# Gates, means and rates land on 64 partitions, and ScalarE copies them to the other 64

## The chip, the cores and the metric

The kernel runs on one core of one Trainium2 chip. Five engines work side by side, each with its own queue of instructions, which it takes strictly in order: TensorE (PE, with its weight loads as PEld), VectorE (DVE), ScalarE (ACT), GpSimd (POOL) and SyncE (SP), which here issues the DMAs. They wait for one another by semaphores. The metric is the device time of one execution in microseconds (us); the time of a kernel is the median of its runs. Profiles come from one profiled execution.

## What is computed

One layer on an image batch x of shape (2, 128, 256, 256), float32: a windowed attention (8x8 windows, keys from 12x12 windows, relative positions, a fixed mask that leaves every second row and column), then a mixture of eight experts for each pixel, of which the two likeliest count.

```
x = x + attention(layernorm over channels(x), W_qkv, W_out, rel_height, rel_width)
t = pixels of x as tokens of 128 channels
n = layernorm(t)
p = softmax(n @ router_w + router_b)                # 8 experts
top_p, top_i = top 2 of p, divided by their sum
t = t + sum over the two of top_p * (n @ expert_w[top_i] + expert_b[top_i])
```

The mask makes the four pixel parities of an image independent, so the attention runs on four "planes" of each strip.

## The kernel before

The image is cut into strips of 8 rows, 64 strips in all. A strip is worked on in four planes, one for each parity of row and column, so the main loop runs over 256 planes, `n`. In each plane it computes the attention of one plane, projects the next one, and does the expert layer for one chunk of 512 pixels (two image rows, "row" in the code) of the strip before. The order of the instructions on all engines is written out by hand in this loop: what stands first in the program stands first in its engine's queue.

**The expert layer of a chunk takes three planes.** In plane n, `norms` squares the chunk (ScalarE, L537), sums it by matmuls (L543), turns the sums (VectorE, L552) and computes the rates (L192 to L199 with two small ScalarE steps, L196 and L197). `route` then finds the two experts and their shares, the gates; its softmax exponential is on ScalarE (L581), and VectorE's next step, L590, needs it. Gates, the means and the rates of the next layer norm have one number for each pixel, but every channel, so every partition, needs them. `spread` writes them to a small DRAM tile `gd` (L622), and DMAs read them back to all 128 partitions by broadcast: `fetch_rstd` (tile `rb`, L628), `fetch_means` (tile `sb`, L657) and `Experts.fetch` (tiles `gb`, L652), each 128 partitions x 512 numbers, 256 KB. In the plane after that, `means` makes xs = x + means (L662), `times` multiplies xs by each gate (L668; experts 5 and 7 on GpSimd, the others on VectorE), and `product` multiplies by the expert's weights on TensorE (L677), all eight summed in one accumulator. `end` adds the accumulator to x (L683).

**The order around the copies.** A gate's buffer comes free when its last reader is done. `fetch` marks that by writing one column of it, on ScalarE or VectorE (L649, L651), and the DMA waits for that mark. In the order of the loop, ScalarE has: the exponential of the scores L462, the values L318, the mark of gate 7, the keys L394 and L404, the queries L410, the two squares L537, the mark for loading x (L116), L196 and L197, the mark of gate 4, L581, the mark of gate 5. SP has, in each plane: gate 7, `gd`, the value rows (L329), `rb`, `sb`, the value windows `vwin` (L341, two DMAs to 60 partitions each, one in each half of the partitions), gates 0, 1, 2, x, gate 3, the finished chunk to DRAM (L715), gates 4, 6, 5. GpSimd has: a copy of one column that makes it wait for gate 6's multiply (`behind`, L672), the multiply of gate 5, the layer norm of a row (`ln1`, L236), sometimes a copy of a halo row (L210), the multiply of gate 7. TensorE has, from the score matmuls (L437, L454) on: the projections of the next plane (L310, L369, L383, L408), products 4, 6, 7, 5 of the chunk before, the attention (L475, L485), the sums L543, products 0, 1, 2, the output projection L513, product 3.

**The start.** For the first six planes (`FILL`) there are no or few expert chunks, and the order is a little different.

**The finish.** `finish_last` does the last four chunks together, on a shorter path: one route for all four (L798 to L849), gates fetched to 128 partitions into buffers of x that are free, multiplies on VectorE, two of eight on GpSimd (L760), products into four parts of one PSUM tile `accs` (L767), adds (L878, L882) and stores.

**Alignment.** `nc.tensor.addr_align` puts idle instructions in TensorE's stream, so that the borders of its instruction blocks (256 instructions) fall at chosen places of the loop.

Of the kernel before, what the change touches and what calls it, by code (L numbers as in the profile page):

```python
# [52 lines left out]
def kernel(  # L53
# [571 lines left out]
    def fetch_rstd(gd, nm):  # L625

        rb = gates.tile([P, NT * P], F32, tag="rb", name=f"rb{nm}", bufs=2)
        nc.sync.dma_start(rb, to_all(gd, E + 1))  # L628
        return rb

    def to_all(gd, j):

        return gd[j * NT : (j + 1) * NT].rearrange("r k -> (r k)").partition_broadcast(P)

    class Experts:
# [7 lines left out]
        def fetch(self, e, eng):  # L643
# [6 lines left out]
            else:  # L650
                eng.memset(self.gb[e][:, 0:1], 0.0)  # L651
            nc.sync.dma_start(self.gb[e], to_all(self.gd, e))  # L652

        def fetch_means(self):

            self.sb = gates.tile([P, NT * P], F32, tag="sb", name="sb%d_%d" % self.at, bufs=1)
            nc.sync.dma_start(self.sb, to_all(self.gd, E))  # L657

# [27 lines left out]
    class NoExperts:  # L686
        def fetch(self, e, eng):
            pass

# [32 lines left out]
    def finish_last(ex, nxt, gated):  # L722
# [27 lines left out]
        def multiply(at, row):  # L750
# [6 lines left out]
            for e in range(E):  # L757
                xe = work.tile([P, CH], F32, tag="xe", name=f"xel{row}_{e}", bufs=8)
                eng = nc.gpsimd if e in (2, 5) and row < 4 else nc.vector
                eng.tensor_tensor(xe, xs, gb[e], ALU.mult)  # L760
                out.append(xe)
            return out

        def products(acc, xes):
            order = (0, 1, 3, 2, 4, 6, 5, 7)
            for j, e in enumerate(order):
                nc.tensor.matmul(  # L767
                    acc, lhsT=ew[:, e, :], rhs=xes[e], start=(j == 0), stop=(j == E - 1)
                )
# [22 lines left out]
        for e in (0, 1, 2, 3, 4, 6, 5, 7):  # L792
            nxt.times(e, nc.gpsimd)
        for e in (0, 1, 2, 3, 4, 6, 5, 7):
# [70 lines left out]

        accs = ps_att.tile([P, 4, CH], F32, tag="att", name="accs")
        todo = [f] + rows
        before = nxt
        for row, at in enumerate(todo):
# [3 lines left out]
            if row == 0:  # L873
                before.end()
                store(*to_store.pop())
            else:
                src = rows_of(*todo[row - 1])
                nc.vector.tensor_add(src, accs[:, (row - 1) % 4], src)  # L878
                store(*todo[row - 1])
            products(accs[:, row % 4], xes)  # L880
        src = rows_of(*todo[-1])
        nc.vector.tensor_add(src, accs[:, (len(todo) - 1) % 4], src)  # L882
        store(*todo[-1])
# [95 lines left out]
    with tc.manual_schedule(engines={ET.PE, ET.DVE, ET.Activation, ET.Pool, ET.SP}):  # L979
        for n in range(n_planes):  # L980
# [11 lines left out]

            usual = n > 6 and row_at(n - 1) is not None
            if usual:
                nc.tensor.addr_align(BLOCK, offset=BLOCK - FIRST_LIMIT)
# [11 lines left out]
            next(ahead, None)  # L1007
            nxt.fetch(7, nc.scalar)
            if gated:
                f, c, made = gated  # L1010
                gd = spread(f, c, made[0], f"_{n}")
                new = Experts(*f, gd) if f else new
# [11 lines left out]
            for e in (4, 6, 7, 5):  # L1024
                ex.product(e)
            if n >= 6 and not usual:
                nc.tensor.addr_align(BLOCK, offset=SUMS_AT)


            f = (i - 1, pl) if 0 < i <= len(strips) else None  # L1030
            c = row_at(n)
            if f or c:
                room = None
# [26 lines left out]
            load_x((n + 9) // 4, (n + 9) % 4, paced=True)  # L1060
            new.fetch(3, dve)
            while to_store:
                store(*to_store.pop())
# [3 lines left out]
            ex.product(1)  # L1067
            ex.product(2)
            new.fetch(4, nc.scalar)
            nxt.behind(6)  # L1070
            nxt.times(5, pool)
# [74 lines left out]
```

## Time and profile before

| what | value |
|---|---|
| median of three runs | 4292.7 us |
| lowest and highest | 4290.45, 4301.58 us |
| the profiled execution | 4302.19 us |
| its span, first to last instruction | 4300.4 us |
| mean granted TensorE clock | 0.994 |
| DMA share of the middle slices | 0.78 to 0.79 |
| data moved by DMA | 1022 MB, mean 238 GB/s |
| DMAs of gates, means, rates | 2008, 251, 249, 256 KB each |
| median from issue to landing | 5.7, 4.3, 3.5 us |
| mean of one multiply of a gate, VectorE, GpSimd | 685, 1272 ns |

Times in the profile are microseconds unless marked ns. A line of the timeline has: start, duration, engine, line of the kernel, operation, output and inputs, partitions x elements, and how many instructions are merged (x8); a bracket at the end gives the idle time of the engine just before and what ended it ("issue": nothing that the profile shows). A DMA line gives the tile, the queue (SPq), how many, the size and the median time from issue to landing. Matmuls of float32 are shown as two instructions each, and matmuls overlap, so a busy TensorE is not TensorE at its peak. Busy shares are averages over the whole span.

### The profile page before, as it was taken

To read this page: it belongs to the slowest core of one execution; us is meant where nothing else is said; L and a number is where in the kernel's file an instruction comes from. 1 tells how busy PE (TensorE), PEld (TensorE's weight loads), DVE (VectorE), ACT (ScalarE), POOL (GpSimd) and SP (SyncE) were. 2 spreads that over 40 slices of the span, in tenths; PEclk is the share of its full clock that TensorE was granted. 3 is DMA by queue.
4 is the path that set the end of the run, shared out by engine and by line. 5 is a ranking of instruction groups with operands and counts; after the bars stand their busy time and mean duration, and the time that the engine had idled before them with its cause. 6 is when DMAs were issued, how large, how long until landed. Compare 5 with 4: busy or idle time off the path is not lost.

```text
span 4300.4 us, 224047 instructions
## 1 busy us (share of the span) xinstructions
PE 4214.7 (98%) x94273; PEld 2457.6 (57%) x94273; DVE 3786.3 (88%) x11752; ACT 1315.5 (31%) x3750; POOL 1093.2 (25%) x1125
## 2 busy tenths in 40 slices
PE   7999999999999999999999999999999999999997
PEld 5555555555555555555555555555555555555553
DVE  5888898998988888998898888989898888888887
ACT  3333333332323232333333333323233333333320
POOL 1222222222222222222222222222222222222222
PEclk9999999999999999999999999999999999999999
DMA  4777777877787877887778787787778787777776
GB/s 141 228 248 238 245 242 244 244 245 243 240 248 233 251 235 234 247 244 242 247 239 249 237 249 239 246 245 244 238 243 249 234 249 238 243 234 247 232 217 198
DMA packets 824576, 1022.15 MB, mean 238 GB/s; under 512 B 137634, under 2 KB 409634, under 8 KB 823594
## 3 DMA queue, kind: packets, MB, share of 16 engines
q1 hardware_dynamic: 822864, 1007.52, 75.7%
q8 instruction: 769, 12.60, 1.3%
q14 instruction: 213, 1.74, 0.1%
q10 hardware_dynamic: 730, 0.29, 0.0%
HBM read 863.78 MB, written 143.75 MB: 234 GB/s over the span
## 4 chain that ended last, share of the span: by engine, by line
PE 97%; issue 1%; DVE 1%; DMA 1%; SPq 0%; ACT 0%; POOL 0%; POOLq 0%; DVEq 0%
PE acc L677 41%; PE att L454 8%; PE att L485 7%; PE pv L310 7%; PE plt L543 6%; PE pu L369 5%; PE po L513 5%; PE pk L383 5%; PE pq L408 5%; PE att L437 4%; PE att L475 3%; DMA gl<-gd_l 1%; PE accs L767 0%; PE pltn L253 0%; DMA xt<-in_x_dram 0%
## 5 line engine op out<-in xcount | busy, mean ns | idle before, releaser
L677 PE MATMUL acc<-xe,ew 128*128 128x512 f32 x4016 | 1880.8, 599 | 10.2 <-issue 8.9
L677 PEld LDWEIGHTS acc<-xe,ew 128*128 128x128 f32 x4016 | 740.9, 190 | 913.0 <-issue 856.3
L668 DVE TENSOR_TENSOR xe<-xs,gb 128x512 f32<-128x512 f32 x1500 | 927.6, 685 | 8.6
L672 POOL COPY last<-xe 128x1 f32<-128x1 f32 x250 | 45.9, 184 | 3042.7 <-DVE gb L651 3042.7
L668 POOL TENSOR_TENSOR xe<-xs,gb 128x512 f32<-128x512 f32 x508 | 645.4, 1272 | 12.2 <-DMA gb<-gd 10.7
L454 PE MATMUL att<-qs,kcol 32*60 32x32 f32 x32768 | 393.9, 222 | 25.2 <-issue 24.7
L454 PEld LDWEIGHTS att<-qs,kcol 32*60 32x60 f32 x32768 | 388.1, 126 | 29.7 <-issue 29.0
L236 POOL TENSOR_TENSOR xn<-xt,rb 128x512 f32<-128x512 f32 x249 | 374.4, 1504 | 87.5 <-DMA rb<-gd 74.2
L485 PEld LDWEIGHTS att<-pT,vwin 64*32 64x32 f32 x32768 | 350.8, 105 | 48.6 <-issue 11.1
L485 PE MATMUL att<-pT,vwin 64*32 64x32 f32 x32768 | 348.7, 201 | 9.1 <-issue 8.4
L462 ACT ACTIVATE pT<-att 128x1024 f32<-128x1024 f32 x256 | 262.0, 1023 | 269.4 <-PE att L454 269.3
L310 PE MATMUL pv<-wt,xn 128*128 128x128 f32 x2048 | 300.3, 290 | 0.0
L537 ACT ACTIVATE sq<-xt 128x512 f32<-128x512 f32 x501 | 290.2, 630 | 0.0
L357 DVE STREAM_TRANSPOSE au<-auT 128x512 f32<-128x512 f32 x256 | 269.5, 1053 | 8.8
L373 DVE STREAM_TRANSPOSE uT<-pu 128x512 f32<-128x512 f32 x256 | 183.2, 716 | 105.2 <-PE pu L369 102.1
L394 ACT COPY kcol<-pk 128x560 f32<-128x560 f32 (+2 forms) x344 | 183.0, 532 | 290.5 <-PE pk L383 287.7
L513 PE MATMUL po<-o,wt 128*128 128x512 f32 x512 | 262.1, 593 | 4.5 <-ACT kcol L404 2.1
L369 PE MATMUL pu<-xn,wrel 128*128 128x512 f32 x512 | 266.0, 601 | 0.0
L408 PE MATMUL pq<-xn,wt 128*128 128x512 f32 x512 | 261.8, 592 | 1.6 <-issue 1.6
L383 PE MATMUL pk<-xn,wt 128*128 128x512 f32 (+2 forms) x528 | 262.4, 580 | 0.0
L310 PEld LDWEIGHTS pv<-wt,xn 128*128 128x128 f32 x2048 | 251.0, 193 | 10.6 <-DVE xn L236 0.2
L437 PEld LDWEIGHTS att<-au,keys 32*64 32x64 f32 x8192 | 116.0, 131 | 195.5 <-PE po L513 189.2
(2445 smaller groups left out, 4935.1 us busy)
## 6 DMA issues: line engine op xcount, KB each, us to landing
gb<-gd SPq DMA_DIRECT2D x2008, 256.0 KB, 5.7
vwin<-vrows SPq DMA_DIRECT2D x512, 240.0 KB, 4.8
xt<-in_x_dram SPq DMA_DIRECT2D x256, 256.0 KB, 6.6
out_dram<-xt SPq DMA_DIRECT2D x256, 256.0 KB, 6.0
sb<-gd SPq DMA_DIRECT2D x251, 256.0 KB, 4.3
rb<-gd SPq DMA_DIRECT2D x249, 256.0 KB, 3.5
vrows<-vr SPq DMA_DIRECT2D x168, 256.0 KB, 3.9
vrows<-vr SPq DMA_DIRECT2D x160, 128.0 KB, 3.4
```

The lines of the kernel that those rows point to most:

```text
L236: eng.tensor_tensor(xn[i % 2][:, :, :, k, 1 : PC + 1], ln1_src(i, k).rearrange("p (y j x) -> p y x j", y=2, x=2), rb.rearrange("p (y j x) ...
L310: nc.tensor.matmul(pv[:, j * P : (j + 1) * P], lhsT=xp[:, k, 1 : PC + 1], rhs=wv, start=True, stop=True,)
L369: nc.tensor.matmul(pu, lhsT=wrel, rhs=inner, start=True, stop=True)
L383: nc.tensor.matmul(pk[:, : m * PC], lhsT=wk, rhs=xp[:, part[0] : part[0] + m, 1 : PC + 1], start=True, stop=True,)
L408: nc.tensor.matmul(pq, lhsT=wq, rhs=inner, start=True, stop=True)
L437: nc.tensor.matmul(sc[rows, h].rearrange("p (t w z) -> p t w z", w=2, z=16)[:, :, w], lhsT=keys[hp, turn, w], rhs=au[hp, half * NP + w : ( ...
L454: nc.tensor.matmul(sc[rows, h, 32 * t : 32 * t + 32], lhsT=kk[hp, half * HP + t, 0:NK], rhs=qs[hp, m0 : m0 + 2].rearrange("p m a s -> p (m ...
L485: nc.tensor.matmul(av[hp, half, 32 * t : 32 * t + 32], lhsT=vv[rows, t, hp], rhs=pT[rows, h, 32 * t : 32 * t + 32], start=True, stop=True,)
L513: nc.tensor.matmul(po, lhsT=wo, rhs=state["o"].rearrange("p f z -> p (f z)"), start=True, stop=True)
L537: nc.scalar.activation(sq, src, AF.Square)
L668: eng.tensor_tensor(self.xe[e], self.xs, self.gb.pop(e), ALU.mult)
L677: nc.tensor.matmul(self.acc, lhsT=ew[:, e, :], rhs=self.xe.pop(e), start=(e == 0), stop=not self.xe)
```

## The change

- `to_all` gets a count, and two helpers are new: `fetch_half` reads to partitions 0 to 63 alone (128 KB), and `other_half` copies those 64 partitions to the other 64 on ScalarE. Rates, means and gates of the main loop go this way. The finish still fetches its gates to 128 partitions.
- The copies are put into ScalarE's order by hand: gate 3 behind the mark of gate 7; gates 4, 6, 5 behind the queries, ahead of the squares; means, rates and gate 7 behind the mark for loading x; gate 0 behind L197, then the mark of gate 4, gates 1 and 2, ahead of L581.
- In the finish, all multiplies are on VectorE, both those of the last regular chunk (before: all eight on GpSimd) and those of the last rows (before: two of eight on GpSimd); the products are in the order of the experts; and each row's products have a PSUM tile of their own in place of a part of `accs`.
- The alignment at a plane's start is kept in one more plane (250).

```diff
@@ -625,12 +625,20 @@
     def fetch_rstd(gd, nm):
 
         rb = gates.tile([P, NT * P], F32, tag="rb", name=f"rb{nm}", bufs=2)
-        nc.sync.dma_start(rb, to_all(gd, E + 1))
+        fetch_half(rb, gd, E + 1)
         return rb
 
-    def to_all(gd, j):
-
-        return gd[j * NT : (j + 1) * NT].rearrange("r k -> (r k)").partition_broadcast(P)
+    def to_all(gd, j, count=P):
+
+        return gd[j * NT : (j + 1) * NT].rearrange("r k -> (r k)").partition_broadcast(count)
+
+    def fetch_half(tile_, gd, j):
+
+        nc.sync.dma_start(tile_[0:SLOT], to_all(gd, j, SLOT))
+
+    def other_half(tile_):
+
+        nc.scalar.copy(tile_[SLOT:], tile_[0:SLOT])
 
     class Experts:
 
@@ -649,12 +657,20 @@
                 eng.copy(self.gb[e][:, 0:1], onesm[:, 0:1])
             else:
                 eng.memset(self.gb[e][:, 0:1], 0.0)
-            nc.sync.dma_start(self.gb[e], to_all(self.gd, e))
+            fetch_half(self.gb[e], self.gd, e)
+
+        def double(self, e):
+
+            other_half(self.gb[e])
 
         def fetch_means(self):
 
             self.sb = gates.tile([P, NT * P], F32, tag="sb", name="sb%d_%d" % self.at, bufs=1)
-            nc.sync.dma_start(self.sb, to_all(self.gd, E))
+            fetch_half(self.sb, self.gd, E)
+
+        def double_means(self):
+
+            other_half(self.sb)
 
         def means(self):
 
@@ -685,6 +701,12 @@
 
     class NoExperts:
         def fetch(self, e, eng):
+            pass
+
+        def double(self, e):
+            pass
+
+        def double_means(self):
             pass
 
         def fetch_means(self):
@@ -756,16 +778,14 @@
             out = []
             for e in range(E):
                 xe = work.tile([P, CH], F32, tag="xe", name=f"xel{row}_{e}", bufs=8)
-                eng = nc.gpsimd if e in (2, 5) and row < 4 else nc.vector
-                eng.tensor_tensor(xe, xs, gb[e], ALU.mult)
+                nc.vector.tensor_tensor(xe, xs, gb[e], ALU.mult)
                 out.append(xe)
             return out
 
         def products(acc, xes):
-            order = (0, 1, 3, 2, 4, 6, 5, 7)
-            for j, e in enumerate(order):
+            for e in range(E):
                 nc.tensor.matmul(
-                    acc, lhsT=ew[:, e, :], rhs=xes[e], start=(j == 0), stop=(j == E - 1)
+                    acc, lhsT=ew[:, e, :], rhs=xes[e], start=(e == 0), stop=(e == E - 1)
                 )
 
         gd = spread(f, None, made[0], "_c")
@@ -790,7 +810,9 @@
         nxt.means()
         ex.end()
         for e in (0, 1, 2, 3, 4, 6, 5, 7):
-            nxt.times(e, nc.gpsimd)
+            if e > 2:
+                nxt.double(e)
+            nxt.times(e, nc.vector)
         for e in (0, 1, 2, 3, 4, 6, 5, 7):
             nxt.product(e)
 
@@ -863,7 +885,7 @@
             2, gds[1], [gates.tile([P, CH], F32, tag="gb", name=f"gl2_{e}", bufs=8) for e in range(E)]
         )
 
-        accs = ps_att.tile([P, 4, CH], F32, tag="att", name="accs")
+        accs = []
         todo = [f] + rows
         before = nxt
         for row, at in enumerate(todo):
@@ -875,11 +897,12 @@
                 store(*to_store.pop())
             else:
                 src = rows_of(*todo[row - 1])
-                nc.vector.tensor_add(src, accs[:, (row - 1) % 4], src)
+                nc.vector.tensor_add(src, accs[row - 1], src)
                 store(*todo[row - 1])
-            products(accs[:, row % 4], xes)
+            accs.append(mm_tile(f"accl{row}"))
+            products(accs[row], xes)
         src = rows_of(*todo[-1])
-        nc.vector.tensor_add(src, accs[:, (len(todo) - 1) % 4], src)
+        nc.vector.tensor_add(src, accs[-1], src)
         store(*todo[-1])
 
     n_planes = 4 * len(strips)
@@ -990,8 +1013,8 @@
 
 
 
-            usual = n > 6 and row_at(n - 1) is not None
-            if usual:
+            late = n == 6 or n > 6 and row_at(n - 1) is None
+            if n > 6 and (not late or row_at(n - 2) is not None):
                 nc.tensor.addr_align(BLOCK, offset=BLOCK - FIRST_LIMIT)
 
 
@@ -1006,6 +1029,7 @@
             next(score, None)
             next(ahead, None)
             nxt.fetch(7, nc.scalar)
+            nxt.double(3)
             if gated:
                 f, c, made = gated
                 gd = spread(f, c, made[0], f"_{n}")
@@ -1023,12 +1047,14 @@
                 next(ahead, None)
             for e in (4, 6, 7, 5):
                 ex.product(e)
-            if n >= 6 and not usual:
+            if late:
                 nc.tensor.addr_align(BLOCK, offset=SUMS_AT)
 
 
             f = (i - 1, pl) if 0 < i <= len(strips) else None
             c = row_at(n)
+            for e in (4, 6, 5):
+                nxt.double(e)
             if f or c:
                 room = None
                 if filling:
@@ -1059,6 +1085,10 @@
                 next(ahead, None)
             load_x((n + 9) // 4, (n + 9) % 4, paced=True)
             new.fetch(3, dve)
+            new.double_means()
+            if row:
+                other_half(row[2])
+            nxt.double(7)
             while to_store:
                 store(*to_store.pop())
             next(ahead, None)
@@ -1066,7 +1096,10 @@
             made = next(norm, None)
             ex.product(1)
             ex.product(2)
+            new.double(0)
             new.fetch(4, nc.scalar)
+            new.double(1)
+            new.double(2)
             nxt.behind(6)
             nxt.times(5, pool)
             if row:
```

## The prediction

> **What bounds the kernel now.** I read the chain of waits first, then the waits, one regular plane on each engine, and the DMA table.
>
> ```profile
> span 4300.4 us, 224047 instructions
> PE 4214.7 (98%) x94273; PEld 2457.6 (57%) x94273; DVE 3786.3 (88%) x11752; ACT 1315.5 (31%) x3750; POOL 1093.2 (25%) x1125
> ...
> PE 97%; issue 1%; DVE 1%; DMA 1%; SPq 0%; ACT 0%; POOL 0%; POOLq 0%; DVEq 0%
> ...
> gb<-gd SPq DMA_DIRECT2D x2008, 256.0 KB, 5.7
> vwin<-vrows SPq DMA_DIRECT2D x512, 240.0 KB, 4.8
> ```
>
> TensorE is the bound, so no removed DMA shortens the path directly. The starts of L437 lie 16.245 us apart in an undisturbed plane. Over the 241 planes between 130 and 4100 us the excess over 16.245 sums to 54 us, with 96 planes over by more than 0.05. Three planes, each with a granted clock of 0.5 for 3.4 us, make 9.5 us of it. Much of the rest is idle time that always falls at the same matmul, ended by "issue":
>
> ```profile
> 2031.23 0.36 PE L454 MATMUL att<-qs,kcol 32*60 32x32 f32 x17
> 2031.78 1.31 PE L454 MATMUL att<-qs,kcol 32*60 32x32 f32 x111 [0.18 <-issue]
> ```
>
> Always with 111 left in L454, 21 in L485 or 5 in L677: edges of instruction blocks (the instruction queue moved 769 packets of 16 KB), whose fetch shares the DMA engines with the gates. So 54 us is the most that steady planes could give back. The question is what the new ScalarE work costs. Here is its row of one plane, without what lies between:
>
> ```profile
> 2000.28 1.02 ACT L462 ACTIVATE pT<-att 128x1024 f32<-128x1024 f32 x1 [0.84 <-PE att L454]
> ...
> 2005.48 0.18 ACT L116 COPY xt<-onesm 128x1 f32<-128x1 f32 x1
> 2012.78 0.18 ACT L196 ACTIVATE r__121_38773<-plg 128x8 f32<-128x8 f32 x1 [7.12 <-DVE plg L195]
> 2012.99 0.21 ACT L197 ACTIVATE r__121_38773<-r__121_38773 128x8 f32<-128x8 f32 x1
> 2013.10 0.17 ACT L649 COPY gb<-onesm 128x1 f32<-128x1 f32 x1
> 2015.29 0.23 ACT L581 ACTIVATE lg<-lg 128x32 f32<-128x32 f32 x1 [2.01 <-DVE lg L580]
> ```
>
> The reader sees two holes: 7.1 us behind L116 and 2.0 us ahead of the router's exponential L581. VectorE has next to none; its only two waits are 0.48 us on ScalarE's L197 and this:
>
> ```profile
> 2015.38 0.16 DVE L584 TENSOR_TENSOR g<-sd,plg 128x4 f32<-128x4 f32 x1
> 2015.55 0.43 DVE L590 TENSOR_TENSOR cmp<-lg 128x256 f32<-128x256 f32 x1
> ...
> 2018.48 0.72 DVE L373 STREAM_TRANSPOSE uT<-pu 128x512 f32<-128x512 f32 x1 [0.22 <-PE pu L369]
> ```
>
> L590 starts the moment L581 is done: a late L581 stops VectorE, which has only 0.22 us a plane to catch up. I call times from the start of L462 "at".
>
> **The change, part by part.** Ten ScalarE copies of 64x512 a plane (eight gates, means, rates). Nearest row: sq L537, 128x512, 0.63 alone, 1.15 for two, so 0.53 each in a row; 10 x 0.53 = 5.3 us, 245 regular planes: 1.3 ms, ScalarE 31% to 61%. By place:
>
> - Gate 3, behind the marker at 1.57 to 1.76: ScalarE waits 1.04 us for pk there (to 2.81), the copy takes 0.53: nothing. Without that cover it would be 0.53 on kcol.
> - Gates 4, 6, 5, ahead of the squares: 1.6 us; squares end at 6.9 (7.3 where kcol takes two parts) and the matmuls that read them start at 8.72: nothing. The gates landed (in the trace's issue and landing records, medians of 171 regular planes) at 2.4, 3.3, 4.4 of this plane; the copies start at 4.2.
> - Means, rates, gate 7, in the 7.1 us hole: means land at 9.99, so three copies end at 11.6; L196 is due at 12.50: nothing, 0.9 us to spare. Behind them on GpSimd, ln1 goes from 9.89 to 11.1 and the multiply of gate 7 ends at 13.9 (14.5 with a halo copy) instead of 12.6; its product is due only in the next plane.
> - Gates 0, 1, 2, in the 2.0 us hole ahead of L581. This is the place. They land at 14.44, 15.40, 16.15 now, and L581 starts at 15.01. Queued behind the waiting copies are gate 4's marker (its DMA, and behind it on SP those of 6, 5, 7), L581, gate 5's marker and the next L462. If landings stay, the copies end at 16.68.
>
> How long a 64-partition transfer takes no row shows. **Low end:** half the packets at the same 84 ns each (the gates' 2 KB packets) halve the 0.65 us that a gate takes at the DMA engines back to back: 0.33. **High end:** vwin, the one transfer that goes to a half only (60 partitions), lands 1.84 us behind its twin for 240 KB, so 128 KB would be 0.98, though its packets are 512 B. I take 0.60, in between and near the 0.65 of now, as vwin is nearer in where it writes. Four such transfers in front (means, gates 0 to 2) and the earlier ones shorten the wait a little: gate 2 at 15.9, copies done at 16.43.
>
> [...]
>
> What a late L581 costs: VectorE can trail TensorE once by the smallest slack between them. The add L683 ends at 8.99 and the product that reuses its accumulator starts at 9.73: 0.74 us (the output projection has 1.0). With that used up, L581 is wanted at 15.01 + 0.74 = 15.75, and a plane longer by d moves that by d; a loss of 0.22 + d must equal 16.43 - 15.75 - d, so d = (16.43 - 15.97) / 2 = 0.23 us. Over 241 planes 55 us; but a plane that VectorE sets hides up to 0.23 of its fetch stall, and the list of excesses gives 20 us hidden. **Steady planes: +36 us.** Ends: landings at 15.5 or earlier give 0; unchanged ones (d = 0.36) give 86 - 28 = +58.
>
> **The finish.** Now a single accumulator tile makes each row's products wait for the add of the row before:
>
> ```profile
> 4261.28 9.47 PE L767 MATMUL accs<-xel,ew 128*128 128x512 f32 x16 [4.23 <-DVE xt L878]
> ...
> 4272.24 7.13 PE L767 MATMUL accs<-xel,ew 128*128 128x512 f32 x16 [1.49 <-DVE xt L878]
> 4280.87 7.13 PE L767 MATMUL accs<-xel,ew 128*128 128x512 f32 x16 [1.49 <-DVE xt L878]
> 4289.39 7.13 PE L767 MATMUL accs<-xel,ew 128*128 128x512 f32 x16 [1.39 <-DVE xt L878]
> ```
>
> Separate tiles free 4.23 + 1.49 + 1.49 + 1.39 = 8.6 us at most of these; rows are also held by their gates' DMAs, the last of which are issued by 4276.5 and take 5.6, so the products could end near 4284 instead of 4296.5. VectorE takes over GpSimd's multiplies: 8 x 0.61 = 4.9 us a row, under the 6.9 of the products. The eight multiplies of the last regular row stand ahead of L798: +4.9, and against that the router's operations are no longer slowed beside GpSimd:
>
> ```profile
> 4237.79 0.98 DVE L820 TENSOR_TENSOR lg_l<-lg_l,rb 128x128 f32<-128x128 f32 x1
> 4238.81 0.29 DVE L821 TENSOR_REDUCE mx_l<-lg_l 128x16 f32<-128x128 f32 x1
> ```
>
> Seven such (L806, L808, L811, L812, L813, L820, L822) are about 5 us over what a neighbour of their size takes: even. Finish: -9 us (0 to -14).
>
> **The start.** In the filling planes the rates' copy stands ahead of L196 (0.5 us in each of five planes), and plane 5 waits for gate 2 (landed at 14.2, L581 at 11.5), partly absorbed: +4 us (0 to +7). The alignment of TensorE's code changes for one plane alone (250): 0.
>
> **Sum:** 4302.2 us (the profiled execution; span 4300.4) + 36 - 9 + 4 = 4333. The median of the runs, 4292.7, is 9.5 us lower; on it, 4292.7 + 31 = 4324.
>
> **Rivals.**
> 1. *Everything fits* (not slower): a transfer takes 0.33. Gates 0 to 2 land 1.3 us earlier (four halved transfers), the copies end by about 15.4, below the 15.97 from which d is 0. The 2 KB packets fill 61% of the DMA engines' time, three quarters of it gates, means and rates; DMA falls from 76% to some 53%, and the 54 us of fetch stalls fall by 16 (in proportion) to 54; I take 35. 4292.7 - 35 - 9 + 4 = 4253. For it: the 84 ns packets; against it: vwin.
> 2. *Same*: landings as forecast, but gate 2 at 15.5 or before; only the ends count: 4288.
> 3. *GpSimd gets into VectorE's way* (slower still): its last multiply now ends at 13.9 to 14.5, and from L577 at 14.34 VectorE has operations with two SBUF inputs, which beside GpSimd took 0.98 in the finish against 0.3. From means landing at about 10.4 (a quarter land after 10.7) it decides; 0.4 us a plane more would be 4324 + 0.2 x 245 to 0.4 x 245 = 4373 to 4422, say 4390. Against it: VectorE's trailing of 0.74 moves L577 to 15.1.
>
> **Chances.** Forecast 0.45, everything fits 0.30, same 0.13, GpSimd 0.12. The forecast's own range is 4295 to 4355. The whole reaches to the middle of the first rival and the third's price: 4245 to 4390. What a measurement can tell from no change is 0.3%, 13 us. Faster by more: all of the first rival and a little of the second, 0.34. Within: most of the second and the forecast's low end, 0.16. Slower: 0.50.
>
> **What would show it.** In the trace after: L581's idle ended by gate copies, its start at 16 or later, L590 waiting for it, TensorE idle ahead of L677 on L683; the 2 KB packets of the gates near 150 ns and not 84. Rival 1: packets of 84 ns, DMA near 53%, fewer "issue" gaps. Rival 3: L577, L580 or L590 long beside GpSimd's L668. I am wrong if gates 0 to 2 land before 15.5, or if VectorE can trail by more than 0.74.

## The result, and the profile after

| | before | after |
|---|---|---|
| median of four runs each, one chip | 4291.57 us | 4343.52 us |
| lowest and highest | 4284.79, 4301.58 | 4334.71, 4347.15 |
| the profiled execution | 4302.19 | 4344.05 |

The ratio is 1.011, 95% interval [1.0094, 1.0127]: 1.1% slower, some 52 us. The new kernel moves 694 MB by DMA instead of 1022 and still loses.

The page of the kernel after: its busy times, the share of the chain that ended last by engine, the costliest groups (line, engine, operation, tile, shapes, count | busy us, mean ns | idle before them and its releaser), and the gates' DMAs.

```profile
span 4342.3 us, 225925 instructions
PE 4240.4 (98%) x94273; PEld 2486.0 (57%) x94273; DVE 3784.9 (87%) x11768; ACT 2778.5 (64%) x6258; POOL 1080.1 (25%) x1109
...
PE 63%; DVE 14%; DMA 11%; issue 7%; ACT 3%; SPq 1%; DVEq 0%
...
L693 PE MATMUL acc<-xe,ew 128*128 128x512 f32 x4016 | 1871.9, 599 | 34.9 <-DVE gb L659 34.4
L641 ACT COPY gb<-gb 64x512 f32<-64x512 f32 x2008 | 1165.7, 614 | 194.1 <-DMA gb<-gd 171.7
...
gb<-gd SPq DMA_DIRECT2D x2008, 128.0 KB
```

Before, the chain was TensorE for 97%. Now TensorE has 63% of it, and VectorE, DMAs, "issue" and ScalarE share the rest. ScalarE went from 31% to 64%; a copy of a gate lasts 614 ns. The gates' DMAs carry 128 KB and not 256, and the page gives no landing time for them. (The products are L677 before and L693 after, the add behind them L683 and L699.)

The waits of the kernel after (who waited for whom: us in total, times, longest):

```profile
ACT gb L641 <- DMA gb<-gd: 171.7, 166, 3.3
DVE cmp L590 <- ACT lg L581: 144.8, 153, 3.2
PE acc L693 <- DVE gb L659: 34.4, 54, 0.9
PE att L437 <- issue: 24.5, 80, 2.4
PE att L454 <- issue: 6.0, 6, 3.2
PE att L485 <- issue: 4.7, 4, 2.3
```

Of the first four only the last was there before, with 0.8 us. They are one story told by three engines: a copy of gate 0, 1 or 2 waits for its DMA, VectorE's L590 waits for the exponential L581 that stands behind the copies, and TensorE waits for VectorE, ahead of product 0 or ahead of the next plane's L437. In the second pair of lines the old stalls at block edges are almost gone; before they were

```profile
PE att L454 <- issue: 24.7, 34, 4.1
PE acc L677 <- issue: 8.9, 20, 0.8
PE att L485 <- issue: 8.4, 15, 2.6
```

That these pauses go with the fetch of instructions can be read from the trace before: TensorE's 196769 instructions came in 769 packets of 16 KB, 256 to a packet, and all 48 of them over 0.25 us with 111 matmuls left in L454 or 21 in L485 end 1.2 to 1.6 us behind the end of such a packet, a stretch that holds 7% of the time.

From the trace, summed over the 240 planes 10 to 249 as spacing of L437's starts over 16.245 us: before 53 us, after 112. So steady planes lost 59. The part from plane 255's start to the last addition went from 89.3 to 77.1 us, the part ahead of plane 10 from 172.1 to 170.8. Planes 250 to 254 took 3.5 us less. 58.8 - 12.2 - 1.3 - 3.5 = 42 us, the difference of the two profiled executions.

Where in a plane it went: means over planes 20 to 245, in ns, each from the first matmul of a block to the first of the next.

| | scores L454 | attention L485 | products 4, 6, 7, 5 | sums L543 to product 0 | product 3 to next L437 |
|---|---|---|---|---|---|
| before | 1542 | 1301 | 3583 | 1011 | 953 |
| after | 1552 | 1314 | 3524 | 1175 | 1073 |

The last two columns are the loss: 164 and 120 ns a plane, which in 240 planes make 39 and 29 us. The products' column is saved fetch stalls (14 us). In the first two columns the stalls went too (from 33 to 11 us), yet the means rose by 10 and 13 ns. For L454 this shows in the median as well, which rose from 1432 to 1550 ns (that of L485 stayed at 1268): something else took the place of the stalls. A little more than one plane of the kernel after, cut to what matters, shows how the loss comes about; start, duration, engine, line, what it does, and idle time before:

```profile
1192.83 0.23 ACT L581 ACTIVATE lg<-lg 128x32 f32<-128x32 f32 x1
1193.09 0.43 DVE L590 TENSOR_TENSOR cmp<-lg 128x256 f32<-128x256 f32 x1 [0.59 <-ACT lg L581]
...
1195.54 0.25 DVE L614 STREAM_TRANSPOSE gT<-g 128x64 f32<-128x64 f32 x1
1195.82 2.35 SPq L622 DMA_DIRECT2D gd<-gT  x2
...
1199.97 0.54 SPq L637 DMA_DIRECT2D sb<-gd  x1
1200.62 1.05 SPq L341 DMA_DIRECT2D vwin<-vrows  x2
1201.79 1.88 SPq L637 DMA_DIRECT2D gb<-gd  x3
...
1207.55 0.62 ACT L641 COPY gb<-gb 64x512 f32<-64x512 f32 x1 [0.91 <-DMA gb<-gd]
...
1208.39 1.14 ACT L641 COPY gb<-gb 64x512 f32<-64x512 f32 x2
...
1209.56 0.23 ACT L581 ACTIVATE lg<-lg 128x32 f32<-128x32 f32 x1
1209.82 0.42 DVE L590 TENSOR_TENSOR cmp<-lg 128x256 f32<-128x256 f32 x1 [0.83 <-ACT lg L581]
```

It is a ring of waits. L581 lets VectorE go on to L614, 2.7 us later; that lets SP write `gd`; `rb`, `sb` and `vwin` stand ahead of gates 0, 1, 2 on SP; these land some 5.7 us after their issue; the copies follow, and behind them stands the next L581, 16.73 us after the last. TensorE needs 16.245. What was a line of steps before (L581 waited for nothing that its own gates set in motion) now closes on itself.

How much a late L581 costs can be read plane by plane. Take the time by which L581 starts behind the first L437 of the next plane, and what that plane loses in the last two columns against 1011 and 952 ns (planes 20 to 245). Before, L581 starts 0.80 us behind L437 (median). In the kernel after it lies between 0.76 and 2.79 us (5th and 95th of a hundred). The 125 planes below 1.5 us lose 5 ns each, the 82 planes from 1.7 us up lose 0.77 us each, 63 of the 65 us in all. So the slack is there and has a sharp edge, some 0.7 to 0.9 us behind the old place; the loss is in the planes that lie beyond it. And the ring passes on only a part of a delay: fitted over these planes, an L581 that is 1 us later goes with `gd` written 0.7 us later, gates 0 and 2 issued 0.35 and 0.66 us later, and the next L581 0.4 us later.

### The profile page after: what moved, and what is told of

It is laid out like the page before. It is cut to its first block, busy times and chain, and to the rows that moved or that the text cites. A ratio compares the mean times of both kernels' runs of the same rounds, so it can differ in the third digit from the quotient of the medians.

```text
span 4342.3 us, 225925 instructions
## 1 busy us (share of the span) xinstructions
PE 4240.4 (98%) x94273; PEld 2486.0 (57%) x94273; DVE 3784.9 (87%) x11768; ACT 2778.5 (64%) x6258; POOL 1080.1 (25%) x1109
## 4 chain that ended last, share of the span: by engine, by line
PE 63%; DVE 14%; DMA 11%; issue 7%; ACT 3%; SPq 1%; DVEq 0%
PE acc L693 27%; DMA gb<-gd 10%; PE att L454 6%; DVE xe L684 6%; PE pv L310 5%; PE att L485 4%; PE pu L369 4%; PE po L513 4%; PE pk L383 3%; PE pq L408 3%; PE plt L543 3%; PE att L437 3%; ACT gb L641 3%; PE att L475 2%; DVE xs L678 1%
## 5 line engine op out<-in xcount | busy, mean ns | idle before, releaser
L693 PE MATMUL acc<-xe,ew 128*128 128x512 f32 x4016 | 1871.9, 599 | 34.9 <-DVE gb L659 34.4
L641 ACT COPY gb<-gb 64x512 f32<-64x512 f32 x2008 | 1165.7, 614 | 194.1 <-DMA gb<-gd 171.7
L693 PEld LDWEIGHTS acc<-xe,ew 128*128 128x128 f32 x4016 | 740.9, 189 | 931.7 <-issue 849.5
L641 ACT COPY sb<-sb 64x512 f32<-64x512 f32 x251 | 154.9, 617 | 652.8 <-DMA sb<-gd 537.7
L454 PE MATMUL att<-qs,kcol 32*60 32x32 f32 x32768 | 415.1, 222 | 6.0 <-issue 6.0
L454 PEld LDWEIGHTS att<-qs,kcol 32*60 32x60 f32 x32768 | 412.3, 126 | 7.5 <-issue 6.6
L485 PEld LDWEIGHTS att<-pT,vwin 64*32 64x32 f32 x32768 | 359.5, 105 | 43.7 <-issue 5.8
L485 PE MATMUL att<-pT,vwin 64*32 64x32 f32 x32768 | 356.4, 200 | 5.1 <-issue 4.7
L462 ACT ACTIVATE pT<-att 128x1024 f32<-128x1024 f32 x256 | 261.7, 1022 | 140.1 <-PE att L454 132.3
L513 PE MATMUL po<-o,wt 128*128 128x512 f32 x512 | 262.5, 594 | 3.3 <-ACT kcol L404 2.1
```

Of the source, the lines that this page charges most:

```text
L454: nc.tensor.matmul(sc[rows, h, 32 * t : 32 * t + 32], lhsT=kk[hp, half * HP + t, 0:NK], rhs=qs[hp, m0 : m0 + 2].rearrange("p m a s -> p (m ...
L485: nc.tensor.matmul(av[hp, half, 32 * t : 32 * t + 32], lhsT=vv[rows, t, hp], rhs=pT[rows, h, 32 * t : 32 * t + 32], start=True, stop=True,)
L513: nc.tensor.matmul(po, lhsT=wo, rhs=state["o"].rearrange("p f z -> p (f z)"), start=True, stop=True)
L641: nc.scalar.copy(tile_[SLOT:], tile_[0:SLOT])
L693: nc.tensor.matmul(self.acc, lhsT=ew[:, e, :], rhs=self.xe.pop(e), start=(e == 0), stop=not self.xe)
```

## The experiments

Each run was timed against the kernel before on the same chip. The kernel before was at 4286.0, 4305.3, 4302.9 and 4303.9 us in the four groups of runs, so ratios are compared, and expectations in us are read against 4286 to 4292. "Excess" is the sum over 240 planes as above, from the profiled execution; "L581" is its median start behind that of L462, all planes (15.02 before).

| run | median us | ratio to before, interval | excess | L581 | L454, L485, to product 0, to L437 (mean ns) |
|---|---|---|---|---|---|
| before | | 1 | 53 | 15.02 | 1542, 1301, 1011, 953 |
| after | 4343.5 | 1.011 [1.0094, 1.0127] | 112 | 15.75 | 1552, 1314, 1175, 1073 |
| move | 4262.8 | 0.9946 [0.9933, 0.9959] | 29 | 15.01 | 1479, 1325, 1016, 956 |
| move_b | 4265.9 | 0.9909 [0.9892, 0.9925] | 33 | 15.05 | 1496, 1319, 1016, 965 |
| whole012 | 4268.2 | 0.9909 [0.9896, 0.9923] | 35 | 14.91 | 1523, 1290, 1011, 962 |
| move_full | 4294.6 | 1.002 [1.0009, 1.0032] | 58 | 15.42 | 1473, 1304, 1072, 1014 |
| finish | 4278.7 | 0.9979 [0.9967, 0.9992] | 29 | 15.01 | 1499, 1293, 1011, 955 |
| wait1 | 4333.0 | 1.0064 [1.0051, 1.0077] | 83 | 15.85 | 1529, 1329, 1055, 1057 |
| after_noalign | 4702.1 | 1.098 [1.0961, 1.0998] | 456 | 15.70 | 1928, 1384, 1665, 952 |
| after_pad | 4353.8 | 1.0111 [1.0097, 1.0125] | 122 | 16.20 | 1550, 1321, 1296, 952 |
| after_early | 4358.4 | 1.0125 [1.011, 1.014] | 120 | 15.76 | 1558, 1315, 1179, 1071 |
| gates_first | 4322.1 | 1.0041 [1.0027, 1.0054] | 91 | 15.22 | 1534, 1531, 1015, 953 |
| move_pad | 4257.4 | 0.9888 [0.9875, 0.9902] | 24 | 14.95 | 1515, 1284, 1014, 952 |
| move_pad_b | 4257.2 | 0.9891 [0.9875, 0.9908] | 25 | 14.95 | 1515, 1286, 1012, 952 |

### Which copies cost

**move**: the kernel after with nothing copied ahead of L581.

```diff
...
             nxt.fetch(7, nc.scalar)
-            nxt.double(3)
+            nxt.double(0)
+            nxt.double(1)
...
-            for e in (4, 6, 5):
+            for e in (2, 3, 4, 6):
                 nxt.double(e)
...
             next(norm, None)
+            nxt.double(5)
...
-            new.double(0)
             new.fetch(4, nc.scalar)
-            new.double(1)
-            new.double(2)
```

> The kernel after, with nothing of ScalarE's copies left ahead of L581: gates 0 and 1 are copied a plane later in the hole behind gate 7's mark (where gate 3 was), gates 2, 3, 4, 6 behind the queries, gate 5 behind the squares; all fetches stay halved, the finish as in the kernel after. Theory (the three copies ahead of L581 are the whole loss: they delay L590, so product 0 waits, and the wait uses up the lead under which the idle instructions ahead of L437 and the block edges of L454 were hidden): L581 starts at 15.1 or before, L590 has no wait on it, the wait ahead of product 0 and the 345 ns ahead of L437 vanish, fetch stalls stay gone, excess of the 240 steady planes 112 -> about 15 us, time 4245 us (4235 to 4262). Rival (ten copies of 64x512 a plane slow the matmuls beside them, wherever they stand): L454's block stays at 1550 ns, excess 60 or more, 4290 to 4330 us.

Measured: 0.9946, and 0.9909 in the second group (move_b, below): faster than both kernels. L581 is back at 15.01, the wait of L590 for it is gone from the list, the stretches to product 0 and to L437 are back at 1016 and 956 ns, excess 29 us. So ten copies a plane cost next to nothing in these places, and the three ahead of L581 were the loss. Part of the gain is the finish's: the run finish below, timed in the same group, took 4278.7 us, and move is 16 us under it. The time is 0.8 us above the range, since the excess is 29 and not 15: L454 and L485 kept part of their slowness (below).

**whole012**: the kernel after, gates 0, 1, 2 fetched whole and not copied, all else in its place.

```diff
+            if e in (0, 1, 2):
+                nc.sync.dma_start(self.gb[e], to_all(self.gd, e))
+            else:
+                fetch_half(self.gb[e], self.gd, e)
...
-            new.double(0)
             new.fetch(4, nc.scalar)
-            new.double(1)
-            new.double(2)
```

> The kernel after, with gates 0, 1, 2 alone fetched to all 128 partitions again and not copied; the other seven stay halved and are copied where the kernel after has them. Theory (the copies of gates 0 to 2 ahead of L581 are the whole loss): L581 at 15.1 or before, no wait ahead of product 0, 4265 us (4258 to 4278; somewhat more DMA than move, so some fetch stalls). Rival (the copies of means, rates and gate 7, whose wait for the landing of the means is 538 us in the kernel after, hold the queue as well): 4300 us or more.

Measured: 0.9909, L581 at 14.91, to product 0 1011 ns. The other seven copies stay where the change put them, means still waiting 454 us in all for their landing, and cost next to nothing. This is the smallest undoing tried that turns the loss into a gain.

**move_full**: as move, with every fetch whole, so the copies write what is there.

```diff
-        nc.sync.dma_start(tile_[0:SLOT], to_all(gd, j, SLOT))
+        nc.sync.dma_start(tile_, to_all(gd, j))
```

> As the run called move, but every fetch goes to all 128 partitions again, so the ten ScalarE copies write what is there already: copies without the lighter DMA load. Theory (the fetch stalls went because the DMA load fell; copies at these places cost nothing): stalls as in the kernel before, excess about 53 us, and the shorter finish: 4280 us (4270 to 4292), DMA 76%. Rival (stalls went for another reason): same as the run move, within 8 us. Rival (copies cost by themselves): 4300 us or more.

Measured: 4294.6 us, 2.6 above the range, excess 58. TensorE's waits at block edges (L454, L485 and the products, ended by "issue") come to 26 us, as in finish (26; before 42), against 10 in move. So the lighter DMA load takes these stalls down. But with the finish's gain this run should have come to 0.998, and most of the 29 us between its excess and that of move is something else: 56 and 58 ns a plane to product 0 and to L437, 27 us. It is the same fault at a second place. With whole fetches the means land later, their copy starts at 10.36 behind L462 (median) and in a quarter of the planes at 11.18 or later, against 9.20 and 9.87 in move; the copies of means, rates and gate 7 need 1.7 us, and L196, due at 12.5, stands behind them: a quarter of the planes has it at 13.21 or later (12.59 before), and L581 is late in its train (15.42). The prediction's third rival has a hand in it: in 77 of 226 planes VectorE's L577 lasts 0.65 us (mean) beside GpSimd's multiply of a gate, against 0.19 in all planes of the kernel before. In 46 of these L196 is late too, 0.76 us behind the L195 that it reads, and the 46 planes hold 26 of the 28 us that the two columns lose. So the three copies are free in the runs with halved means and not in this one.

**finish**: the kernel before with the edits of the finish alone.

```diff
-                eng = nc.gpsimd if e in (2, 5) and row < 4 else nc.vector
-                eng.tensor_tensor(xe, xs, gb[e], ALU.mult)
+                nc.vector.tensor_tensor(xe, xs, gb[e], ALU.mult)
...
-            nxt.times(e, nc.gpsimd)
+            nxt.times(e, nc.vector)
...
-        accs = ps_att.tile([P, 4, CH], F32, tag="att", name="accs")
+        accs = []
...
+            accs.append(mm_tile(f"accl{row}"))
```

> The kernel before with the edits of the finish alone (one PSUM tile for each row's products, all multiplies on VectorE, order of experts). Theory: the finish gains by itself, 89.3 -> 77 us behind the last plane, 4279 us (4276 to 4284), steady planes unchanged at an excess of 53 us. Rival (the 12 us that the finish of the kernel after is shorter come from its lighter DMA load or from its copies in the last planes): 86 us or more, 4288 to 4292 us.

Measured: 76.8 us from plane 255's start to the last addition, against 89.3. The medians differ by 7 us, and the ratio, 0.9979, makes it 9. The finish gains by itself. Its rows' products in the kernel after, TensorE, with what they waited for:

```profile
4300.01 16.82 PE L787 MATMUL accl<-xel,ew 128*128 128x512 f32 x32 [8.39 <-DVE xel L781]
4317.51 20.87 PE L787 MATMUL accl<-xel,ew 128*128 128x512 f32 x48 [0.68 <-DVE xel L781]
```

No row waits for the add of the row before any more; five rows run in two blocks. (This run's steady planes, the same code as before, have an excess of 29 in this execution and before 53, of which 16 us is less waiting at block edges, 26 against 42; three planes with a stretch at a granted clock of 0.5 hold 9.5 us more before, and here there is none. So much do executions differ.)

### How late L581 may be

**wait1**: the kernel before with one ScalarE copy of a single column of gate 1's tile ahead of L581. It makes L581 wait for that landing, and nothing else.

```diff
+        def landed(self, e):
+
+            nc.scalar.copy(seen, self.gb[e][:, 0:1])
...
             new.fetch(4, nc.scalar)
+            for e in (1,):
+                new.landed(e)
```

> The kernel before, unchanged but for one ScalarE copy of a single column of gate 1's tile (0.18 us) between the mark of gate 4 and L581 in every plane: L581 then waits for gate 1's landing at 15.40 and starts at about 15.6, 0.6 later, with no 64x512 copy and no halved fetch. The prediction's step (VectorE can trail TensorE by 0.74 us, so L581 costs nothing up to 15.75): 4284 to 4294 us, no wait ahead of product 0. Rival (the real slack is some 0.2 us, as the 0.345 us ahead of L437 in the kernel after suggest, and L581 0.45 late is enough): both waits appear in most planes, 4325 to 4370 us.

Measured: 1.0064, 28 us over the 4305.3 of its group. L581's median is 15.85, not 15.6, and a tenth of the planes have it at 16.77 or later. The waits of this kernel:

```profile
ACT seen L688 <- DMA gb<-gd: 601.1, 248, 4.9
...
DVE cmp L590 <- ACT lg L581: 147.2, 181, 3.0
```

L590 waits 147 us for L581, as long as in the kernel after (145), with no 64x512 copy in the kernel at all. So a wait for a landing is enough; the work of copying is not needed for it. The loss lies between the two expectations, nearer the rival's. Plane by plane, "nothing up to 15.75" held: the 117 planes with L581 less than 1.5 us behind L437 lose 5 ns each, the other 109 lose 0.30 us. What did not hold is that L581 would stand at 15.6 in every plane.

**after_pad** and **move_pad**: the 31 idle instructions (71 ns each, 2.2 us of TensorE's sequencer) that stand ahead of L437 are moved behind products 4, 6, 7, 5.

```diff
-            if n > 6 and (not late or row_at(n - 2) is not None):
-                nc.tensor.addr_align(BLOCK, offset=BLOCK - FIRST_LIMIT)
...
-            if late:
+            if n >= 6:
                 nc.tensor.addr_align(BLOCK, offset=SUMS_AT)
```

> The kernel after, with the 31 idle instructions of each plane moved from the plane's start to behind the products 4, 6, 7, 5 (offset 40 there instead of 157 at the start; two of the three block edges of a plane stay where they were, that in L485 moves 16 matmuls ahead). Theory (the idle instructions stand in the open ahead of L437 since product 0 came late): the 345 ns there vanish, the wait ahead of product 0 stays at 36 us, 4343 -> 4316 us (4308 to 4325). Rival (VectorE sets these planes and what is gained ahead of L437 is waited again ahead of product 0): 4335 to 4345 us with a wait ahead of product 0 of 55 us or more.

> The run move with the idle instructions moved in the same way. Theory (the 47 ns that L454's block is longer in move than in the kernel before are the sequencer's small lead behind the idle instructions): L454 back from a mean of 1479 to 1435 ns, 4252 us. Rival (the longer blocks of L454 and L485 come from DMA writes that land beside them): L454 stays near 1479, 4258 to 4267 us.

after_pad: 1.0111, the same as after. The wait ahead of L437 is gone (952 ns) and comes back ahead of product 0 (1296 ns instead of 1175; its wait on VectorE is 60 us, and was 34). VectorE may now trail further: no plane with L581 less than 1.7 us behind L437 loses more than 0.05 us, and those from 1.7 to 2.0 lose 13 ns each (after: 0.24 us). But L581 goes from 15.75 to 16.20, and there is no gain. The rival holds: VectorE sets these planes, and where TensorE spends the wait is of no matter. That idle train was visible in the kernel after, but not its cause.

move_pad: L454 did not come back to 1435 ns but went to 1515; L485 fell to 1284. The theory of a small lead behind the idle instructions is wrong as I had it, and the rival's 1479 was not measured either. The time was 4257; to compare it with move, both ran again on one chip.

> The kernel of the run move again, beside the next one on one chip: 4255 to 4266 us.

> The kernel of the run move_pad again, beside move on one chip. Theory (in move the idle instructions ahead of L437 are hidden, so their place is worth nothing): within 4 us of move_b. Rival (the place is worth the 5 us between their profiled executions): 4 to 10 us below move_b.

4265.9 (4259.3 to 4270.9) and 4257.2 (4255.1 to 4259.3): 8.7 us, the rival's range. move_pad is the best version found: 0.9891 [0.9875, 0.9908] of the kernel before.

**after_noalign**: the kernel after without the idle instructions.

```diff
-                nc.tensor.addr_align(BLOCK, offset=BLOCK - FIRST_LIMIT)
+                pass
```

> The kernel after without the idle instructions at each plane's start (the other alignment stays for its few planes). Theory (31 idle instructions of 71 ns stand in the open ahead of L437 in 75 to 84 of 226 planes, 27 us, because TensorE's sequencer has lost its lead; with a DMA load of 59% the block edges need no chosen place): no 345 ns ahead of L437, steady excess 112 -> 80 us, 4315 us (4305 to 4330). Rival (the edges' place still matters): fetch stalls come back at new places, 4340 us or more.

Measured: 4702 us. The theory missed by far, and the rival holds. Three of the waits of TensorE in it:

```profile
PE plt L543 <- issue: 125.1, 47, 4.8
PE att L454 <- issue: 89.8, 73, 2.8
PE pv L310 <- issue: 15.2, 11, 1.8
```

With the edges of the instruction blocks where they fall, one stall is up to 4.8 us long, though DMA is at 53%. The place of an edge decides, not the DMA load alone. The stalls are not the whole loss. The granted clock of TensorE is 0.968 in this execution, against 0.996 in the kernel after: in the steady planes the profile has 61 stretches with a granted clock of 0.5, most of them 3.4 us long, where the kernel after has none, and the 61 planes with such a stretch hold 301 us of the excess of 456. TensorE's waits on "issue" come to 252 us in the eleven costliest groups of matmuls of this run; at the edges in the kernel after they are 11 us.

### What closes the ring

**after_early**: the kernel after with eleven gate tiles for eight, and VectorE's marks of gates 0, 1, 2 ahead of its multiplies.

```diff
...
+            for e in (0, 1, 2):
+                new.fetch(e, dve)
             for e in (0, 1, 2, 3):
                 nxt.times(e, dve)
-            new.fetch(0, dve)
             for e in (4, 6):
                 nxt.times(e, dve)
-            new.fetch(1, dve)
             ex.end()
-            new.fetch(2, dve)
```

> The kernel after with eleven gate tiles in place of eight, and VectorE's marks of gates 0, 1, 2 ahead of its multiplies (at about 4.7 and not 7.1 to 9.6): their DMAs no longer wait for VectorE and are issued right behind vwin, the copies stand where the kernel after has them. Theory (a ring: late L581 -> late L590 -> late multiplies -> late marks of gates 1 and 2, whose DMAs are issued 0.10 us behind the mark in half the planes -> late landing, 5.7 us after the issue -> late copies -> late L581; VectorE's trailing behind TensorE buys nothing in it): gate 2 is issued near 8.9 and not 9.6 to 9.8, L581 starts by 15.2, 4280 us (4260 to 4300). Rival (the DMA engines are the bound there, so an earlier issue lands no earlier): issue to copy grows from 5.7 to 6.5 us, L581 stays near 15.5, 4325 us or more.

Measured: 1.0125, no better than after. The marks came at 4.7 us behind L462, and gates 0, 1, 2 were issued at 8.14, 8.71, 9.36 (medians, planes 20 to 245), against 8.14, 9.06, 9.70 in the kernel after. So the marks did hold gates 1 and 2, by 0.35 us, but to be rid of them gained nothing: the copies start where they did (gate 1's, which waits for its landing, at 14.55 and 14.58; from issue to copy it is 6.0 us instead of 5.7). That is the rival's sign, an earlier issue that lands no earlier, at a third of its size. Gate 0 was held by no mark but by SP's queue: `gd` written late, its landing waited for by `rb`, then `sb`, then `vwin`. In the kernel after L581 goes with the issue of `vwin` in the same plane (correlation 0.73).

**gates_first**: after_early with gates 0, 1, 2 ahead of `vwin` on SP.

```diff
+            for e in (0, 1, 2):
+                new.fetch(e, dve)
             if n + 1 < n_planes:
                 take_values(n + 1)
-            for e in (0, 1, 2):
-                new.fetch(e, dve)
```

> The run after_early with the DMAs of gates 0, 1, 2 ahead of the two of vwin on SP; the ScalarE copies stay ahead of L581. Theory (the ring closes over SP's queue: from one L581 to VectorE's L614 2.71 us, to the write of gd 3.21, to vwin's second DMA 8.44, to gate 2's DMA 10.18, to the end of its copy 16.4, which is the next L581, 16.45 us later; the marks are no part of it, since after_early issued no gate earlier): gates 0 to 2 go out 1 us or more earlier, gate 2's DMA is issued by 9.0 behind L581, the ring is shorter than a plane, L590 has no wait, 4270 us (4255 to 4290). Rival (the landing of gates 0 to 2 is held by the DMA engines and not by the issue): gate 2's issue to the next L581 grows from 6.3 to 7.3 us, 4330 us or more.

Measured: gate 2 is issued at 7.95 behind L462, 1.4 us earlier than in after_early and 1.75 earlier than in the kernel after; L581 starts at 15.22; L590's wait for it is gone from the list, to product 0 1015 and to L437 953 ns. The waits are gone, as the theory said, with the copies still ahead of L581. More than half of what the issue gained was lost again on the way: gate 0 is issued 1.5 us earlier than in the kernel after, but its copy, which waits for the landing in all 226 planes, starts 6.5 us after the issue instead of 5.7, and from gate 2's issue to L581 it is 7.3 us, the rival's own figure. What is left, 0.6 us, is enough. But the time is 1.0041, not 0.995: the attention's matmuls now take 1531 ns a plane instead of 1314, 52 us in 240 planes. Groups of TensorE in gates_first (busy us, mean ns of one):

```profile
L454 PE MATMUL att<-qs,kcol 32*60 32x32 f32 x32768 | 410.9, 222 | 5.1 <-issue 5.0
L485 PE MATMUL att<-pT,vwin 64*32 64x32 f32 x32768 | 409.2, 200 | 5.4 <-issue 5.0
```

and in the kernel before:

```profile
L454 PE MATMUL att<-qs,kcol 32*60 32x32 f32 x32768 | 393.9, 222 | 25.2 <-issue 24.7
L485 PE MATMUL att<-pT,vwin 64*32 64x32 f32 x32768 | 348.7, 201 | 9.1 <-issue 8.4
```

One matmul lasts as long as before by this view (200 to 222 ns, with ends that the profile models); L485 is busy 60 us longer, so its matmuls start later behind one another (last section). So half of the theory is shown (that an earlier issue of the gates removes the waits) and its time is not, for a reason that is not the ring's.

## Why the prediction was right, and where not

The direction, the place and the chain of waits held; the time came out 19.5 us above the 4324 predicted, inside the forecast's own 4295 to 4355.

- **Where the loss is: right.** Copies of gates 0 to 2 wait, L581 is late, L590 waits, TensorE waits ahead of product 0. All four were named. whole012 and move undo it alone. The sign that I gave, L581 "at 16 or later", was too strong: its median is 15.75, a quarter of the planes 16.29 or later.
- **Steady planes +36: 59. Of its three terms one was near, one too small, one missing.** The waits on VectorE (d, 0.23 us a plane, 55 us) are 164 + 120 ns, 0.28 us a plane, 68 us. The fetch stalls that it would hide were put at 20 of 54; 31 of 42 us of waits at edges went. They were not only hidden behind VectorE: in move, where VectorE holds nothing up, they are 10 us too. Slower blocks of L454 and L485, some 28 us (2 and 3 us longer in all, though 22 us of stalls went from them), had no term.
- **"VectorE can trail TensorE once by 0.74 us", with L581 wanted at 15.75: right as a slack, wrong in what it was fed.** In single planes a late L581 is free up to some 0.7 us, as said above. But the sum gave every plane one landing, fixed in TensorE's time, and gate 2's at 15.9. Its copy starts at 15.13 (median), seldom after a wait, so it lands earlier than that, and the copies end at 15.74, not 16.43. By the prediction's own sum that costs nothing, and by its own sign ("wrong if gates 0 to 2 land before 15.5") it was wrong here. The loss comes from the spread: in 91 of 226 planes the copies end after 15.97. And the landing is not fixed: `gd` is written behind L590, so a late VectorE makes the next gates later in part (gates 0 and 2 by 0.35 and 0.66 us for 1 us, above). More slack (after_pad) was used up by an L581 that came later still. That the sum came out near is in part luck.
- **"The output projection has 1.0" of slack: wrong.** 1.0 us is what lies between the end of VectorE's L505 and the first matmul of L513 (before, median), but in no plane of the kernel after is it under 0.33, so that at most 0.67 was slack. In the 84 planes where L437 comes late behind its 31 idle instructions it is 0.34: there L513 has waited for VectorE. By after_pad this place is worth nothing in the kernel after.
- **The other seven copies cost nothing: right** (whole012). The third rival's sign is there, but it does not decide: L577 lasts 0.4 us or more beside GpSimd's multiply in 31 planes (up to 1.03 us; before, in none). In these planes L581 starts 1.2 us behind L580 (median), so the copies hold it and not L577. In move_full it counts (above).
- **A transfer at 0.60, between 0.33 and 0.98: my estimate, and no run shows it**, since the profile after gives no landing time. The 2 KB packets have a median of 86 ns, as at the low end and not near 150 as I expected, a tenth 171 or more (before 84 and 124). Gates 0 and 1, whose copies waited for their landing in 225 of 226 planes, were copied 5.7 us after their issue; before they had landed 5.7 and 6.2 us after it with twice the bytes. So half the bytes saved 0 and 0.5 us of these two; gate 2's landing, 6.5 before, is only known to be under 5.65. Why the first two saved so little, no run shows. Over the whole run the packets' share of the DMA engines' time fell from 61% to 42%.
- **Finish -9 (0 to -14): right**, -12 in the profiled executions, -7 to -9 by the times of its own run.
- **Start +4: not seen** (-1.3); runs that leave the start alone begin plane 10 at 172 to 176 us, so nothing of this size can be told.
- **The first rival, everything fits at 4253:** not this kernel, but move_pad, with the copies elsewhere, runs at 4257. It expected the three copies to fit ahead of L581, and in two planes of five they did not. Its signs were there in part: packets of 86 ns and fewer "issue" gaps, but DMA at 61% in the middle of the run and not 53.

## What to carry to other kernels

Before putting work that waits for a DMA ahead of another instruction in an engine's queue, follow what that instruction sets in motion: if the chain leads back to the same DMA, in the next round, a delay comes back in part (here 0.4 of it), and more slack against another engine need not help (after_pad). Count the ring's length, issue order of the DMA queue included, against the round. Hold a slack against the spread of the landings and not against their median: here the median plane fits and two planes in five pay. A wait that is seen on the bounding engine is not yet its cause: move it and see whether the time follows.

## What the runs showed of the hardware that I had not expected

- **Blocks of small matmuls took longer in the kernels whose fetches go to 64 partitions, and much of it was short pauses that went with the issue of a gate's DMA.** The median of L454's time in a plane is 1430 to 1451 ns in the kernels with whole fetches (before, finish, wait1, move_full) and 1471 to 1555 ns in those with halved ones (after and the seven other kernels here, whole012 among them). At 50 ns that is 12 us a run, at 100 ns 24. A part is pauses: from one matmul's start to the next, from the 18th of the 128 on, no step of L454 lasts 60 to 230 ns in the four kernels with whole fetches (planes 20 to 245); in the halved ones 10 (move) to 186 (after_pad) do. In gates_first L485 has 334 such steps, 193 ns a plane, where after has 61, 29 ns: most of the 217 ns by which the block is longer. 97% of the 334 begin 0.10 to 0.25 or 0.70 to 0.90 us after SP starts the issue of a gate's DMA, windows that hold 16% of the time from the 18th matmul on (in the kernel after, the same windows have 91% of L454's 175 such steps and 25% of the time). While L485 runs there, some 9 packets of 2 KB of halved fetches are in flight; before, 10 of whole fetches are. No run here shows whether operands or instructions come late in the pauses. Why a halved fetch goes with pauses stays open: no run separates the halving from the place of the transfers in time.
- **The place of instruction block edges is worth 358 us in this kernel** (4343.5 to 4702.1), more than all else that was tried, the stretches of half clock included; 31 idle instructions a plane, 71 ns each, 2.2 us of the sequencer, buy it, and in move and move_pad they are nearly free.
- **move_pad's times lie closer together:** 4255 to 4259 us in four runs of its second group, where the kernel before went from 4298 to 4312 in seven. That fewer fetch stalls are the reason was not tested.
